# Weighting rows of experts' outputs, and half of the normalised rows, on ScalarE in a four-layer kernel

## The chip, the cores and the metric

The kernel runs on one core of one Trainium2 chip, in one launch. The metric is the device time of that launch in microseconds (us), as the median of several runs. A core has five engines with a queue each, which run in order: PE (TensorE, matrix products and transposes), DVE (VectorE), ACT (ScalarE), POOL (GpSimd) and SP (SyncE, here for issuing DMAs). They meet only through semaphores.

## What is computed

The input x has 2 sequences of 1024 tokens with 128 channels, in float32. Four layers follow each other; every one does the same thing with its own two branches:

```
xn = layernorm(x)                      # no scale, no shift
s  = mixer(xn)                         # layer 0: Mamba-2, 1: delta rule, 2: linear attention, 3: two Mamba-2, one reversed
g  = silu(experts(xn))                 # a mixture of experts
x  = x + s * g
```

The layer norm takes the mean and the variance of a token's 128 channels and gives (x - m) / sqrt(v + 1e-5). In the experts of layers 1 to 3 each token goes to the two experts with the largest logits out of 8, 8 and 16, and the result is their two outputs weighted by the softmax over these two logits. Layers 1 and 3 add a shared expert; layer 2 runs a softmax attention ahead of its experts. Layer 0 computes all 8 experts for all tokens.

## The kernel before, in words

The tokens lie in 16 tiles of 128 (one token to a partition), and four tiles make a group: G = 4, NG = 4. Arrays such as `x`, `xn`, `acc`, `h`, `s` are kept whole in SBUF as 128 partitions x 16 tiles x 128 channels; `grp(a, g)` is one group of them, 128 x 512 elements.

**Normalisation.** `Kern.normalise` (L320) does it for layers 0, 1 and 2, a loop of its own in `layer3` (L1684) for layer 3. For every group `moments` (L303) takes BATCH_NORM_STATS (L310) and BATCH_NORM_AGGREGATE (L311) per tile on DVE, which gives mean and variance in `mv`; `rsqrt` (L296) makes the reciprocal root `rs` by one small DVE operation (L299), a square root on ACT (L300), and a reciprocal on DVE (L301). Layers 2 and 3 also take mean squares (L317, L318). Then DVE writes the four rows of the group, one tile of 128 x 128 each, as (x - m) * rs (L328, in layer 3 L1688). The group is stored to a list in DRAM for the experts (`keep_rows`, L1257, on SP; layers 1 and 3), transposed by PE (L293) and copied from PSUM to `xT` by ACT or DVE in turn (L282, L284). In layer 2 ACT scales the rows for the attention (`xw`, L1381) and POOL turns them (L1389 to L1394); in layer 3 ACT scales them as `xw` (L1696), POOL copies part of that (L1697), and POOL multiplies weights (L1674) at the beginning. In layer 0 ACT takes sums of squares of the same rows (L336).

**Experts of layers 1 to 3.** `Dispatch` (L1134 on) sorts the 4096 pairs of token and expert into blocks of one expert each. The mixers' work and the blocks of rows share the engines: a block's rows are gathered from DRAM (`load`, POOL), put through its expert, and scattered to a list `ys` in DRAM (`store`, L1236, POOL), in which every token has a place for its first and one for its second expert. At the end of the layer `Dispatch.fetch` brings them back. Per group and per k (first or second expert) SP loads a tile `yt` of 128 x 4 x 128 (L1247), after all stores; four buffers take turns. Then `add_scaled` runs for each of the four rows on DVE (L414):

```
self.nc.vector.scalar_tensor_tensor(acc[:, i, :], out, w, acc[:, i, :], ALU.mult, ALU.add)
```

that is, acc = y * w + acc, with w one weight per token. `acc` holds the shared expert's output in layers 1 and 3 and `h`, the attention's, in layer 2. After `fetch` the layer's end follows for the group: a silu on ACT (L1005, L1129, L1808), a product with s on DVE (L1006, L1130, L1809), and the sum with x on DVE (L1007, L1131, L1810). In layer 3 SP then writes the output (L1811). The chunks of the state space of layer 3 (`StateSpace.unit`, L540 on: exponentials `uE` and `ueA` on ACT, products on DVE and POOL, among them L632, L640 and L597) run beside its last fetch.

**Order.** Each engine's order is made when the program is built, by a planner that runs the instructions through a model of their times and takes what is ready first. Only PE's order in the attention of layer 2 is written out by hand. Tiles come from pools; a tile of a pool that reuses memory waits for the last reader of what lay there.

Of the kernel before, what the change touches and what calls it, by code (L numbers as in the profile page):

```python
# [10 lines left out]
F32 = mybir.dt.float32  # L11
F32R = mybir.dt.float32r
I32 = mybir.dt.int32
AF = mybir.ActivationFunctionType
ALU = mybir.AluOpType
# [4 lines left out]
P = 128  # L20
# [4 lines left out]
G = 4  # L25
# [247 lines left out]
class Kern:  # L273
# [29 lines left out]
    def moments(self, pool, src, n, eps, tag):  # L303
# [8 lines left out]
        self.rsqrt(rs, mv[:, :, 1], 1.0, eps)  # L312
        return mv, rs

    def mean_squares(self, out, mv, rs):

        self.nc.vector.tensor_mul(out, mv[:, :, 1], rs)  # L317
        self.nc.vector.tensor_mul(out, out, rs)  # L318

    def normalise(self, pool, ps, x, xn, xT, xs=None, ms=None):  # L320

        for g in range(NG):
            mv, rs = self.moments(pool, lambda j: x[:, g * G + j, :], G, 1e-5, "ln")
            if ms is not None:
                self.mean_squares(ms[:, g * G : (g + 1) * G], mv, rs)
            for j in range(G):
                i = g * G + j
                self.nc.vector.tensor_scalar(xn[:, i, :], x[:, i, :], mv[:, j, 0:1], rs[:, j : j + 1], ALU.subtract, ALU.mult)  # L328
            if xs is not None:
                keep_rows(self, xs, xn, g)  # L330
            self.to_feature_major(ps, lambda i: xn[:, i, :], xT, g)
# [72 lines left out]
    def logits(self, pool, ps, xT, w, bias, E):  # L404
# [3 lines left out]
        lg = pool.tile([P, NT, E], F32, name="lg", tag="lg")  # L408
        self.nc.vector.tensor_add(lg, pl, bias.unsqueeze(1).to_broadcast([P, NT, E]))
        return lg  # L410

    def add_scaled(self, acc, i, out, w):

        self.nc.vector.scalar_tensor_tensor(acc[:, i, :], out, w, acc[:, i, :], ALU.mult, ALU.add)  # L414

# [248 lines left out]
def grp(a, g):  # L666
    return a[:, g * G : (g + 1) * G, :]
# [466 lines left out]
class Dispatch:  # L1134
# [106 lines left out]
    def fetch(self, pool, acc, g, weights):  # L1241

        nc, tc = self.K.nc, self.K.tc
        slots = self.ys.rearrange("(k i p) d -> p k i d", k=2, p=P)
        for k, wk in enumerate(weights):
            y = pool.tile([P, G, P], F32, name="yt", tag="yt", bufs=4)
            d = nc.sync.dma_start(y, slots[:, k, g * G : (g + 1) * G, :])  # L1247
            for q in self.out:
                tc.add_manual_dep(d.ins, q.ins.name, mybir.DependencyInfo(mybir.DependencyClass.Sync, mybir.DependencyReason.DATA), reason="slots of any block")
            for j in range(G):  # L1250
                i = g * G + j
                self.K.add_scaled(acc, i, y[:, j, :], wk[:, i : i + 1])


def keep_rows(K, xs, src, g):

    K.nc.sync.dma_start(xs.rearrange("(i p) d -> p i d", p=P)[:, g * G : (g + 1) * G, :], grp(src, g))  # L1257
# [396 lines left out]
def layer3(K, x, xn, xT, w, inp, out):  # L1654
    nc, tc, c = K.nc, K.tc, K.c
    four = [P, G, P]
    with ExitStack() as es:
        pa = es.enter_context(tc.tile_pool(name="a3", bufs=1))
        pf = es.enter_context(tc.tile_pool(name="f3", bufs=1))
# [21 lines left out]
        rs = pa.tile([P, NT], F32, name="ars")  # L1681
        xs = inp["lists"][0]
        pl = sf.tile([P, NT, 20], F32, name="plg", tag="ps")
        for g in range(NG):  # L1684
            mv, r = K.moments(pf, lambda j: x[:, g * G + j, :], G, 1e-5, "ln")
            for j in range(G):
                i = g * G + j
                nc.vector.tensor_scalar(xn[:, i, :], x[:, i, :], mv[:, j, 0:1], r[:, j : j + 1], ALU.subtract, ALU.mult)  # L1688
            keep_rows(K, xs, xn, g)
            gr = rs[:, g * G : (g + 1) * G]  # L1690
            K.mean_squares(gr, mv, r)
            K.rsqrt(gr, gr, 1.0, 1e-5)
            xw = tmp.tile([P, G, 192], F32, name="xw", bufs=2)
            for j in range(G):
                i = g * G + j
                nc.scalar.activation(xw[:, j, :P], xn[:, i, :], AF.Copy, scale=rs[:, i : i + 1])  # L1696
            nc.gpsimd.tensor_copy(xw[:, :, P:], xw[:, :, :64])  # L1697
            K.to_feature_major(sf, lambda i: xn[:, i, :], xT, g)
            b, l0 = g * G // TPB, g * G % TPB * P
            for swap in range(2):  # L1700
                pt = sa.tile(four, F32, name="tpx", tag="ps")
                for j in range(G):
                    nc.tensor.transpose(pt[:, j, :], xw[:, j, 64 * swap : 64 * swap + P], c["ident"])
                pt = pt.rearrange("p a b -> p (a b)")
                up, down = pt[:64], pt[64:]
                if swap:
                    m = min(512, SEQ - 1 - l0)
                    K.copy(X[0][64:, b, l0 + 3 : l0 + 3 + m], down[:, :m])
                    m = 0 if l0 else 1
                    K.copy(X[1][:64, b, l0 + m - 1 : l0 + 511], up[:, m:])  # L1710
                else:
                    K.copy(X[0][:64, b, l0 + 2 : l0 + 514], up)
                    K.copy(X[1][64:, b, l0 : l0 + 512], down)
            for i in range(g * G, g * G + G):
                K.mm(pl[:, i, :], xT[:, i * P : (i + 1) * P], wr)
# [73 lines left out]
        acc = pa.tile([P, NT, P], F32, name="acc", tag="acc")  # L1789
# [24 lines left out]
def build(tc, io, packs):  # L1814
    nc = tc.nc
    with ExitStack() as ctx:
        pool = ctx.enter_context(tc.tile_pool(name="const", bufs=1))
        x = pool.tile([P, NT, P], F32, name="x")
        src = io["x"].rearrange("b (t p) d -> p (b t) d", p=P)
        for g in range(NG):  # L1820
            nc.sync.dma_start(grp(x, g), src[:, g * G : (g + 1) * G, :])
        xn = pool.tile([P, NT, P], F32, name="xn")
        xT = pool.tile([P, T], F32, name="xT")

        def load(into, n, by=nc.scalar):
            t = into.tile([P, packs[n].n], F32, name="w_" + n)
            by.dma_start(t, io[n])
            return View(t, packs[n])

        K = Kern(tc, load(pool, "c"))  # L1830
        dram = ctx.enter_context(tc.tile_pool(name="lists", bufs=1, space=DRAM))
        lists = {n: dram.tile([rows, P], F32, name=n) for n, rows in (("xs", T), ("ys", 2 * T))}
        views = {}
        with tc.tile_pool(name="const0", bufs=1) as pool0:
            w0 = load(pool0, "l0")
            e0 = load(pool0, "e0")
            layer0(K, x, xn, xT, w0, e0)
        later = ctx.enter_context(tc.tile_pool(name="const3", bufs=1))
        views["l3"] = load(later, "l3")
        pair = lists["xs"], lists["ys"]  # L1840
        with tc.tile_pool(name="const2", bufs=1) as pool0:
            views.update((n, load(pool0, n)) for n in ("l1", "l2"))
            layer1(K, x, xn, xT, views["l1"], {"rows": io["rows1"], "lists": pair, **{n: io[n] for n in ("sw1", "sw3", "sw2")}})
            layer2(K, x, xn, xT, views["l2"], {"rows": io["rows2"], "lists": pair})
        layer3(K, x, xn, xT, views["l3"], {"load": lambda pool: load(pool, "x3", nc.sync), "rows": io["rows3"], "lists": pair}, io["out"].rearrange("b (t p) d -> p (b t) d", p=P))
# [17 lines left out]
```

## Time and profile before

| | |
|---|---|
| median of three runs | 1351.3 us (1349.75 to 1352.39) |
| the profiled execution | 1358.85 us, its span 1357.1 us |
| instructions | 19084 |
| mean granted clock of PE | 0.887 of full speed |
| busy PE / DVE / ACT / POOL | 1132.7 / 872.6 / 632.0 / 421.5 us |
| L328, rows normalised, layers 0 to 2 | 48 on DVE, 397 ns each in the mean |
| L1688, the same in layer 3 | 16 on DVE, 516 ns each in the mean |
| L414, rows weighted and added | 96 on DVE, 16 to 32 to a form, medians 339 to 343 ns |
| L1247, loads of yt | 24 of 256 KB, 3.2 us from issue to landing in the median |

The profile is that of one execution, so its time is set against its own span and not against the median. Busy is the time in which an engine executes something; an engine can be idle because it waits, and the profile gives for each group of instructions what ended the idle time ahead of it. The timeline gives, per row: start, duration, engine, line and operation, `out<-in` by the names of the tiles, shape, how many in a row, and in brackets how long the engine was idle before and what released it. Durations overlap within one engine's queue[...].

Where things lie in the span, in us: layer 0 from 0 to 219, layer 1 to 472 (its fetch from 442), layer 2 to 1108 (normalisation 477 to 497, fetch from 1090), layer 3 to the end (normalisation 1105 to 1135, fetch from 1312).

### The profile page before, as it was taken

How to read it: one execution, taken by the hardware profiler on the slowest of the kernel's cores; microseconds unless marked ns; L12 is line 12 of the kernel's file. 1: busy time of each engine (PE TensorE's matmuls, PEld its weight loads, DVE VectorE, ACT ScalarE, POOL GpSimd, SP SyncE). 2: the span in 40 equal slices, each digit the busy share in tenths (PEclk: the TensorE clock that was granted, in tenths of full speed). 3: DMA queues.
4: the chain of work that ended last, by engine and by line, in shares of the span. 5: the costliest groups of instructions: out<-in, count | busy, mean ns of one | idle time of the engine just before them, and what ended most of it. 6: DMA issues, size and time to landing. Idle time of an engine off the chain costs nothing. (4 is left out here: it accounts for less than half of the span.)

```text
span 1357.1 us, 19084 instructions
## 1 busy us (share of the span) xinstructions
PE 1132.7 (83%) x6813; PEld 790.6 (58%) x6813; DVE 872.6 (64%) x2128; ACT 632.0 (47%) x1050; POOL 421.5 (31%) x427
## 2 busy tenths in 40 slices
PE   5699876889899658999998998569989919799995
PEld 2367465788799325544444443347768815477674
DVE  6536445775664886677777661977776477665456
ACT  7664925214612342345556576234353325355661
POOL 0352161036454260000000000034766511377743
PEclk9799886799799967799999989869999958799997
DMA  2000003025344200000000000023345430233411
GB/s 90 0 0 1 1 15 116 8 88 160 99 142 107 63 0 0 1 1 1 1 1 16 9 1 1 8 91 103 127 125 160 131 105 24 70 94 104 65 53 47
DMA packets 49039, 75.71 MB, mean 56 GB/s; under 512 B 7335, under 2 KB 36402, under 8 KB 48688
## 3 DMA queue, kind: packets, MB, share of 16 engines
q1 hardware_dynamic: 39632, 54.30, 12.8%
q0 software_dynamic: 8448, 14.98, 5.0%
q10 hardware_dynamic: 864, 5.21, 1.1%
q8 instruction: 54, 0.88, 0.3%
q14 instruction: 41, 0.34, 0.1%
HBM read 63.95 MB, written 12.85 MB: 57 GB/s over the span
## 5 line engine op out<-in xcount | busy, mean ns | idle before, releaser
L1226 POOL DMA_INDIRECT xb<-xs,dfrom x132 | 132.7, 1005 | 567.9 <-DVE gsum L1291 377.1
L1453 DVE TENSOR_REDUCE mx<-pm 128x1 f32<-128x512 f32 (+3 forms) x304 | 181.9, 655 | 66.1 <-PE pm L287 63.7
L1497 ACT ACTIVATE pr<-psc 128x1024 f32<-128x1024 f32 x144 | 139.5, 1021 | 95.8 <-PE psc L287 67.3
L1236 POOL DMA_INDIRECT ys<-yb,dto x132 | 134.9, 1022 | 86.4 <-DVE yb L1124 35.5
L287 PE MATMUL pm<-kT,qT 32*128 32x128 f32 (+3 forms) x576 | 120.3, 369 | 16.2 <-DVE mx L1453 12.5
L287 PEld LDWEIGHTS pm<-kT,qT 32*128 32x128 f32 x576 | 70.2, 207 | 69.5 <-DVE mx L1453 49.0
L287 PE MATMUL p<-xbT,tw 128*128 128x256 f32 x368 | 98.4, 385 | 3.5 <-ACT sg L1117 3.2
L1117 ACT ACTIVATE sg<-p,tw 128x256 f32<-128x256 f32 x92 | 41.0, 472 | 93.6 <-PE p L287 90.5
L287 PE MATMUL pat<-pr,va 128*32 128x512 f32 x576 | 81.7, 635 | 0.2 <-ACT pr L1497 0.2
L293 PE MATMUL tp<-w_c,xn 128*128 128x128 f32 x64 | 20.5, 421 | 71.8 <-DVE xn L328 44.2
L287 PEld LDWEIGHTS p<-xbT,tw 128*128 128x128 f32 x368 | 62.3, 190 | 14.8 <-ACT sg L1117 5.5
L287 PE MATMUL psc<-qT,kT 32*128 32x512 f32 x288 | 64.7, 496 | 2.8 <-ACT pr L1497 2.7
L1118 DVE SCALAR_TENSOR_TENSOR hh<-p,tw,sg 128x256 f32<-128x256 f32 x92 | 42.3, 475 | 38.4 <-ACT sg L1117 32.9
L287 PEld LDWEIGHTS po<-tw,hh 128*128 128x128 f32 x368 | 54.2, 191 | 10.3 <-issue 3.1
L293 PEld LDWEIGHTS tp<-w_c,xn 128*128 128x128 f32 x64 | 11.8, 190 | 80.2 <-DVE xn L328 28.1
L287 PE MATMUL po<-tw,hh 128*128 128x128 f32 x368 | 56.1, 275 | 1.6 <-DVE yb L1124 1.2
L287 PE MATMUL psc<-mT,onesR 32*128 32x512 f32 x288 | 54.1, 416 | 0.0
L282 ACT COPY xbT<-pxb 128x256 f32<-128x256 f32 (+3 forms) x39 | 15.6, 399 | 64.8 <-PE pxb L813 45.7
L287 PEld LDWEIGHTS psc<-qT,kT 32*128 32x128 f32 x288 | 30.6, 191 | 15.6 <-ACT pr L1497 13.1
L287 PE MATMUL pcum<-kv,w_c 128*128 128x512 f32 x64 | 35.8, 660 | 3.5 <-DVE prod L1317 3.1
L287 PE MATMUL pd<-uda,w_c 128*128 128x512 f32 x64 | 35.2, 652 | 0.9 <-ACT usz L533 0.9
L561 POOL TENSOR_TENSOR uda<-w_c,vdA 128x512 f32<-128x512 f32 x20 | 20.6, 1041 | 48.4 <-PE pd L287 47.6
(523 smaller groups left out, 2787.3 us busy)
## 6 DMA issues: line engine op xcount, KB each, us to landing
tw<-in_rows SPq DMA_DIRECT2D x23, 836.0 KB, 4.7
tw<-in_rows SPq DMA_DIRECT2D x39, 384.0 KB, 3.6
yt<-ys SPq DMA_DIRECT2D x24, 256.0 KB, 3.2
tw<-in_rows SPq DMA_DIRECT2D x47, 128.0 KB, 2.3
xb<-xs,dfrom POOLq DMA_INDIRECT x132, 3.2
ys<-yb,dto POOLq DMA_INDIRECT x132, 2.3
xs<-xn SPq DMA_DIRECT2D x8, 256.0 KB, 2.3
w_l<-in_l ACTq DMA_DIRECT2D x1, 1890.0 KB, 11.2
```

The lines of the kernel that those rows point to most:

```text
L282: self.nc.scalar.copy(out, in_)
L287: self.nc.tensor.matmul(out, lhsT=lhsT, rhs=rhs, start=start, stop=stop)
L293: self.nc.tensor.transpose(pt[:, j, :], src(g * G + j), self.c["ident"])
L561: pool.tensor_mul(da, upto.unsqueeze(1).unsqueeze(1).to_broadcast(lay), m["dA"][:, i0 + j : i0 + j + per, :].unsqueeze(3).to_broadcast(lay))
L1117: nc.scalar.activation(sg, p1[:, k - k0, :], AF.Silu, bias=t[:, 1536 + k : 1537 + k])
L1118: nc.vector.scalar_tensor_tensor(hh[:, k, :], p2[:, k - k0, :], t[:, 1540 + k : 1541 + k], sg, ALU.add, ALU.mult)
L1226: self.K.nc.gpsimd.indirect_dma_start(dst, None, self.xs, bass.IndirectOffsetOnAxis(self.of_token[:, n : n + 1], 0))
L1236: d = self.K.nc.gpsimd.indirect_dma_start(self.ys, bass.IndirectOffsetOnAxis(self.to[:, n : n + 1], 0), src, None, bounds_check=2 * T - 1, ...
L1453: nc.vector.tensor_reduce(mx[:, starts.index(a), g, j : j + k], tile[0][:, : k * m].rearrange("p (j m) -> p j m", m=m), AX.X, ALU.max)
L1497: K.nc.scalar.activation(pr, ps, AF.Exp, scale=scale)
```

## The change

A new function `normal_rows` writes a group's rows. It first makes `off` = -m * rs, a tile of 128 x 4, on DVE. Rows 0 and 2 of the group stay on DVE as before. Rows 1 and 3 go to ACT, as Identity with the scale rs and the bias off, one value each per partition. It serves all four layers.

In `fetch` ACT now multiplies each of the four rows of `y` by its weight, in place, and one DVE addition of 128 x 512 adds the whole tile to the group of acc. `add_scaled` goes.

```diff
+    def normal_rows(self, pool, xn, x, g, mv, rs):
+
+        nc = self.nc
+        off = pool.tile([P, G], F32, name="lnoff", bufs=2)
+        nc.vector.scalar_tensor_tensor(off, mv[:, :, 0], -1.0, rs, ALU.mult, ALU.mult)
+        for j in range(G):
+            i = g * G + j
+            if j % 2:
+                nc.scalar.activation(xn[:, i, :], x[:, i, :], AF.Identity, bias=off[:, j : j + 1], scale=rs[:, j : j + 1])
+            else:
+                nc.vector.tensor_scalar(xn[:, i, :], x[:, i, :], mv[:, j, 0:1], rs[:, j : j + 1], ALU.subtract, ALU.mult)
...
@@ normalise
-            for j in range(G):
-                i = g * G + j
-                self.nc.vector.tensor_scalar(xn[:, i, :], x[:, i, :], mv[:, j, 0:1], rs[:, j : j + 1], ALU.subtract, ALU.mult)
+            self.normal_rows(pool, xn, x, g, mv, rs)
...
-    def add_scaled(self, acc, i, out, w):
-
-        self.nc.vector.scalar_tensor_tensor(acc[:, i, :], out, w, acc[:, i, :], ALU.mult, ALU.add)
...
@@ Dispatch.fetch
             for j in range(G):
                 i = g * G + j
-                self.K.add_scaled(acc, i, y[:, j, :], wk[:, i : i + 1])
+                nc.scalar.activation(y[:, j, :], y[:, j, :], AF.Copy, scale=wk[:, i : i + 1])
+            nc.vector.tensor_add(grp(acc, g), grp(acc, g), y)
...
@@ layer3
-            for j in range(G):
-                i = g * G + j
-                nc.vector.tensor_scalar(xn[:, i, :], x[:, i, :], mv[:, j, 0:1], r[:, j : j + 1], ALU.subtract, ALU.mult)
+            K.normal_rows(pf, xn, x, g, mv, r)
```

## The prediction, made before the changed kernel ran

> **What bounds the kernel now.** I read the page first (PE busy 83% of the span, DVE 64%, ACT 47%), then the chain of waits. That chain can be followed back only to 1104 us, about 19% of the span, so for the rest I read each place that the change touches by itself: first the busy time by stage, then the timeline inside the stage. The changed lines run in seven stages: the normalisations of layers 0 to 3 (L328, L1688) and the fetches of layers 1 to 3 (L414). Columns: stretch, its length, then busy us of PE, PEld, DVE, ACT, POOL, then granted clock, DMA share, GB/s.
>
> ```profile
> 0.00:40.00 40.00, 24.65 (x74) 12.28 (x74) 27.02 (x92) 27.44 (x71) 2.38 (x9) 0.96 0.23 76
> 222.00:245.00 23.00, 17.20 (x58) 13.30 (x59) 15.19 (x71) 18.05 (x42) 0.00 (x0) 0.57 0.49 169
> 449.00:472.00 23.00, 13.53 (x64) 8.23 (x64) 20.66 (x54) 7.47 (x12) 4.40 (x5) 0.96 0.17 47
> 478.00:500.00 22.00, 9.55 (x27) 5.36 (x28) 18.34 (x75) 9.29 (x29) 13.18 (x20) 0.50 0.00 0
> 1090.00:1109.00 19.00, 0.00 (x0) 0.00 (x0) 15.14 (x53) 3.14 (x5) 0.14 (x2) 0.50 0.56 172
> 1109.00:1136.00 27.00, 18.42 (x84) 15.79 (x84) 20.35 (x75) 13.16 (x37) 9.77 (x11) 0.57 0.14 40
> 1312.00:1337.00 25.00, 18.70 (x129) 14.38 (x128) 22.07 (x59) 10.68 (x16) 8.63 (x7) 0.93 0.37 106
> ```
>
> The three fetches (449, 1090, 1312) and the normalisations of layers 2 and 3 (478, 1109) are DVE's: it is busy 75 to 90% of them, ACT 17 to 49%. The normalisations of layers 0 and 1 are not: ACT is at 18.05 of 23 us in layer 1, and in layer 0 it runs from 18.4 to 40 us almost without a gap. The timeline of layer 1 shows what it does there, and who waits:
>
> ```profile
> 236.34 1.28 ACT L874 ACT_TABLE_LOAD   x1
> ...
> 242.63 0.69 DVE L885 TENSOR_TENSOR vb<-vb,beta 128x512 f32<-128x512 f32 x1 [1.14 <-ACT beta L877]
> ```
>
> The tail, from the last fetch to the end, in the timeline:
>
> ```profile
> 1315.53 1.14 DVE L414 SCALAR_TENSOR_TENSOR acc<-yt,rw,acc 128x128 f32<-128x128 f32 x4 [2.62 <-DMA yt<-ys]
> ...
> 1329.73 2.40 DVE L414 SCALAR_TENSOR_TENSOR acc<-yt,rw,acc 128x128 f32<-128x128 f32 x4
> ...
> 1333.89 0.73 DVE L632 SCALAR_TENSOR_TENSOR uy<-uxs,w_l,py 128x512 f32<-128x512 f32 x1
> ...
> 1334.77 1.98 PE L287 MATMUL py<-uE,uxdt 128*64 128x128 f32 x16 [3.23 <-DVE uy L632]
> ```
>
> DVE stands 2.6 us for the first fetched rows, then runs without a gap to 1336; its L414 rows stand in front of uy L632, and PE waits 3.23 us for that one on the way to the end.
>
> **What each operation costs.** From the groups by form (mean ns in the fourth place from the end):
>
> ```profile
> L414 DVE SCALAR_TENSOR_TENSOR h<-yt,rw,h 128x128 f32<-128x128 f32 x16 | 4.7, 344 | 7.2 <-DMA yt<-ys 7.2
> L1006 DVE TENSOR_TENSOR acc<-acc,WT 128x512 f32<-128x512 f32 x4 | 2.8, 692 | 2.3 <-ACT acc L1005 2.3
> L1696 ACT ACTIVATE xw<-xn,ars 128x128 f32<-128x128 f32 x16 | 5.1, 391 | 1.7 <-DVE ars L301 1.5 <-DVE lnrs L301 0.2
> L516 ACT ACTIVATE uxs<-px,w_l 128x512 f32<-128x512 f32 x16 | 12.1, 778 | 0.7 <-PE px L287 0.6
> L478 ACT ACTIVATE uxs<-px,w_l 128x512 f32<-128x512 f32 x24 | 16.3, 687 | 17.0 <-PE px L287 16.9
> ```
>
> Instructions of one engine overlap, so in a queue the distance counts. Four L414 rows take 1.14 us: (1.14-0.34)/3 = 0.265 each. Four L1696 rows take 1.28 us: 0.295 each. The group's add is L1006's shape: 0.69 alone, 0.60 in a row (L1131 at 1099.80, next instruction at 1100.40). A normalised row on DVE is 0.26 (four L328 in 1.11). The same row on ACT, with scale and bias per partition, is not in the trace: L1696 has one such operand, and a second costs 0.09 (L516 against L478), so 0.48 alone and 0.385 in a row. It could be as low as L1696's 0.295; I take 0.385.
>
> Here a rule speaks against the change. The Trainium skill, ScalarE: Activation LUTs, Rules for kernel authors, gives multiplying and adding to VectorE, not ScalarE. By the rows it is right on price: 0.295 against 0.265, so a layer's 32 weightings cost ACT 9.4 us where DVE paid 8.5. By the rule the change loses wherever ACT is full, 0.9 us a layer and the adds on top. By the stages, ACT has 14 to 16 us idle in each fetch, and what counts is what DVE no longer does.
>
> **Fetch, layers 1 to 3.** Per layer DVE loses 32 x 0.265 = 8.5 us and gets 8 adds x 0.60 = 4.8: 3.7 less. ACT gets 9.4. No DMA is added. A yt buffer is held until the add (about 1.28+0.7 us after landing instead of 1.14), so the later four of eight loads on SP's queue are issued about a microsecond later.
> Layer 1: nothing in the stage waits for yt (issued at 442.13, median landing 3.2, first used at 449.27), ACT is 32% busy, and DVE goes on after x at 472.36 with casts that wait for nothing else. So the saving passes on, less new waits of adds for ACT: **-3.0**, from 0 to -3.7.
> Layer 2: DVE runs from 1093.47 to 1108.3, 14.8 us, and layer 3 starts behind it. Now ACT sets the pace: 32 x 0.295 + three silus at 0.55 = 11.1, then add 0.7, silu 0.7, mul 0.7, add 0.7: 14.0. The last yt loads, held longer, may add some: **-0.5**, from -1.5 to +1.5.
> Layer 3: the same 3.7 from a DVE that is full from 1315.5 to 1336, at the end of which PE waits for L632. On ACT the scalings stand ahead of exps, silus and copies of the state space, and wait for the landing that DVE now waits 2.6 us for. Next late behind DVE is POOL's uE product, which ends at 1331.5, some 2.4 us before L632 starts. So **-2.5**, from -3.7 to +1.
>
> **Normalisation.** Per group of four rows DVE loses 2 x 0.26 and gets the offset: L317's shape, 0.09 in a row. That is 0.43 less, 1.7 a layer; ACT gets 2 x 0.385, 3.1 a layer. The rows on ACT wait for the offset, and whatever ACT has behind them (copies, sums of squares, table loads) waits too.
> Where POOL works, DVE's rows are dearer:
>
> ```profile
> 1111.74 3.04 DVE L1688 TENSOR_SCALAR xn<-x,lnmv,lnrs 128x128 f32<-128x128 f32 x4
> 1112.39 1.80 POOL L1674 TENSOR_TENSOR bwst<-w_x 128x768 f32<-128x768 f32 x1
> ```
>
> Four rows take 3.04 instead of 1.11, with one L1674 on POOL from 1110.63 and this one behind it. The Trainium skill, SBUF — State Buffer, Who interferes with whom, says that such a DVE operation and a POOL operation exclude each other, that an operation with two SBUF inputs is caught too while POOL reads, and that ACT never waits. By the first and last points the two ACT rows are worth up to (3.04-1.11)/2 = 1.0 us a group here. By the middle one the offset itself, through which both ACT rows go, is caught: L318 of that size took 0.71 at 490 us. I go by that row, and take less than half.
> Layer 2: the rows of groups 2 and 3 take 3.6 and 2.7 us (487.9, 493.9) between POOL's rotations; two fewer save up to 1.5 and 0.7 after the offset. DVE is the stage's engine and PE waits for its rows: **-1.5**, from -2.5 to +0.5.
> Layer 3: group 0 is held by the two L1674 either way, group 2 (1.99 us) gains 0.8, the others 0.2 each; ACT's xw rows come 0.8 later per group: **-0.5**, from -2 to +2.
> Layer 1: six rows fall into ACT's gap-free stretch, 2.3 us; half of it is covered, as PE's last transposes (242.15) stand behind its logits anyway: **+1.2**, from 0 to +2.3. If that cover goes, it is the whole 2.3.
> Layer 0: the same, with the first group waiting for data at 5.4 and 9.9 us, and DVE's convolutions ending the stretch: **+0.5**, from -0.5 to +2.3.
>
> **Sum:** -3.0-0.5-2.5-1.5-0.5+1.2+0.5 = -6.3 us. The profiled execution took 1358.85 us (span 1357.1), 7.6 above the median of the runs, 1351.3. The difference goes over unscaled: 1352.5 on the profiled execution, **1345.0** on the median. The order within each queue is made by a planner from its own durations, and new instructions can shift it anywhere outside layer 2's hand-ordered PE stretch; I give that 3 us either way, most of this forecast's own range, 1341 to 1348.6. About 0.2%, 2.7 us, is what a measurement here can tell from no change.
>
> **Rivals.**
> (B) All of DVE's time shows, POOL's hold on the rows as well: -3.7-3.7-0.8-2.5-1.5 with layers 0 and 1 at nothing, -12.2: 1339. For it: DVE's 90% in two fetches. Against: ACT's pace in layer 2, and the latency of two engines in place of one. 0.10.
> (C) The saving is hidden: next late is the landing of yt, ACT's silu, or POOL's product, and the ACT terms cancel the rest: 1351, within 2.7. For it: DVE already waits 2.3 us for silu in layer 1's fetch. Against: no DMA wait there at all. 0.22.
> (D) Slower: ACT's queue becomes the bound. Its place is the gap-free stretches of layers 0 and 1 (+2.3 each), layer 3's xw rows (+1.5), layer 2's fetch (+1.5), and the tail, where a scaling waits up to 2.6 us for yt with the exps and copies of the state space behind it (+1.0 net); layer 1's fetch and layer 2's normalisation still give -1.5-1.0. Sum +6.1: 1357.4. It decides from the point where the ACT terms pass the 8.0 us that my DVE terms give. Against it: 51 to 83% of ACT idle in five of seven stages, and Copy and Identity rows that stand in the trace behind other functions with no table load. 0.20.
> The forecast has 0.48. Faster is B and the forecast, 0.58; same 0.22; slower 0.20. The range, 1339 to 1356.5, leaves out half of B and a good part of D.
>
> **What would show it.** DVE's busy time falls by some 18 us (3 x 3.7 + 4 x 1.7), ACT's rises by about 40 with the same number of table loads. From the first yt use to x the fetch of layer 1 shortens by 3, that of layer 2 by under 1; PE's wait for L632 shrinks. Layer 1's normalisation to its first DVE wait for beta lengthens by about 1. I am wrong if ACT waits for yt with state-space work behind it, if table loads multiply, or if a stretch that the change doesn't touch moves by more than 3 us.

## The result, and the profile after

The changed kernel is slower: 1364.57 us in the median of 15 runs (1360.7 to 1372.02), against 1355.1 us (1349.64 to 1363.55) for the kernel before in 15 runs taken with it. The ratio is 1.007 with an interval of [1.0051, 1.0089]. The forecast was 1345.0 us, and its range ended at 1356.5. It started from 1351.3 us for the kernel before, the median of three runs; against the 1355.1 of this comparison the change costs 9.5 us, where 6.3 us less was forecast.

The profiled execution of the changed kernel took 1363.79 us, its span 1362.0 us (before: 1358.85 and 1357.1). Its line numbers are shifted: in layer 1's and 3's fetch L1258 is the weighting on ACT and L1259 the group's add on DVE; L323 is a normalised row on ACT. From its page, the busy time per engine and the chain that ended last by engine:

```profile
PE 1136.2 (83%) x6813; PEld 789.4 (58%) x6813; DVE 854.8 (63%) x2040; ACT 667.2 (49%) x1175; POOL 420.9 (31%) x427
...
PE 55%; DVE 19%; ACT 14%; issue 5%; POOL 4%; DMA 3%; SPq 0%; DVEq 0%; POOLq 0%; ACTq 0%
```

DVE lost 17.8 us of busy time and ACT gained 35.2, close to the 18 and 40 of the prediction (three table loads of 1.28 us fewer are part of the difference in ACT's). So the work went where it was meant to go, at about the price that was put on it. The groups by form of the changed kernel say the same:

```profile
L1258 ACT ACTIVATE yt<-yt,rw 128x128 f32<-128x128 f32 x48 | 15.2, 389 | 12.9 <-DMA yt<-ys 12.9
L323 ACT ACTIVATE xn<-x,lnoff,lnrs 128x128 f32<-128x128 f32 x32 | 14.0, 484 | 4.3 <-DVE lnoff L319 4.3
```

The first line also shows 12.9 us in which ACT stood idle for the landing of `yt`. Most of it, 9.35 us, is in layer 2's fetch, where ACT has nothing else to do; 3.18 us are in layer 1's and 0.34 us in layer 3's, and there other work of ACT stands behind these rows.

Where the time went, in us, by stretches between named instructions of the two traces. `TT` is the first triangular factor of layer 1 (DVE), `pk` layer 2's first key product, `px` layer 3's first state-space product, `pinv` the product from which `Dispatch` takes its list of places (the last three PE):

| stretch | before | after | predicted | measured |
|---|---|---|---|---|
| layer 1 normalisation (last x of layer 0 to the first TT) | 34.36 | 30.96 | +1.2 | -3.4 |
| layer 1 fetch (first yt load to the last x) | 30.23 | 34.44 | -3.0 | +4.2 |
| layer 2 normalisation (first statistics to the first pk) | 20.54 | 19.34 | -1.5 | -1.2 |
| layer 2 attention | 289.17 | 291.77 | 0 | +2.6 |
| layer 2 fetch (last ys store to the last x) | 20.03 | 19.85 | -0.5 | -0.2 |
| layer 3 normalisation (x to the first px) | 28.13 | 26.57 | -0.5 | -1.6 |
| layer 3, px to the last pinv | 30.54 | 32.58 | 0 | +2.0 |
| layer 3 tail (first yt load to the last x) | 41.02 | 44.80 | -2.5 | +3.8 |

The spans differ by +4.9. The table adds up to some +6.3, layer 0 as a whole is 2.2 us shorter (217.4 against 219.6, forecast +0.5), and the rest differs by under a microsecond. The two stretches with the wrong sign are the fetches of layers 1 and 3. First their busy time by stage, of the kernel before (columns as in the prediction):

```profile
442.10:472.40 30.30, 20.18 (x96) 12.14 (x94) 25.23 (x73) 10.88 (x19) 5.56 (x5) 0.96 0.25 70
...
1312.50:1353.50 41.00, 27.58 (x168) 22.91 (x166) 29.10 (x77) 13.58 (x20) 13.56 (x10) 0.79 0.23 67
```

and of the changed one:

```profile
436.30:470.70 34.40, 22.97 (x95) 13.85 (x93) 21.80 (x49) 22.46 (x53) 5.27 (x5) 0.90 0.22 62
...
1313.60:1358.40 44.80, 30.21 (x176) 24.30 (x175) 26.53 (x53) 23.67 (x53) 14.29 (x11) 0.80 0.21 61
```

DVE (third pair) is busy 3.4 and 2.6 us less, about the 3.7 forecast, and yet each stretch is longer. No engine is busy throughout: ACT (fourth pair) is at 65% and 53%. So engines wait, and the timeline must show for what. Layer 1's fetch, before:

```profile
445.09 1.28 ACT L300 ACT_TABLE_LOAD   x1
...
446.62 0.18 DVE L301 RECIPROCAL lors<-lors 128x4 f32<-128x4 f32 x1 [2.23 <-ACT lors L300]
...
449.27 1.96 DVE L414 SCALAR_TENSOR_TENSOR acc<-yt,rw,acc 128x128 f32<-128x128 f32 x4
```

and after:

```profile
439.08 1.28 ACT L1258 ACTIVATE yt<-yt,rw 128x128 f32<-128x128 f32 x4 [2.18 <-DMA yt<-ys]
...
441.82 0.57 ACT L856 ACTIVATE sg<-pgt 128x512 f32<-128x512 f32 x1
442.41 1.28 ACT L300 ACT_TABLE_LOAD   x1
...
443.94 0.18 DVE L301 RECIPROCAL lors<-lors 128x4 f32<-128x4 f32 x1 [5.41 <-ACT lors L300]
...
446.90 1.28 ACT L856 ACT_TABLE_LOAD   x1
...
448.81 1.28 ACT L300 ACT_TABLE_LOAD   x1
```

The first load of `yt` is issued at 436.27. In the kernel before, its first reader ran 7.1 us after the issue (442.13 to 449.27), and 4.3 us after the landing (444.96). In the changed kernel the planner puts the first weighting on ACT 2.8 us after it, so ACT stands 2.18 us for the landing, then weights eight rows, and only then come the shared expert's silu (`sg`) and the square root of the delta rule's last norm. DVE waits 5.41 us for that root instead of 2.23. From there the order of silus and roots on ACT alternates: after 442.41 it loads a function table three times more (446.90, 448.81, 450.32), where before it did so once (449.61).

The tail, in the kernel before. ACT's copy `uBt` feeds PE's state product `pst`; the state space's output products `py` come behind it:

```profile
1320.67 0.59 ACT L588 COPY uBt<-pt 128x512 f32<-128x512 f32 x1 [0.64 <-PE pt L583]
...
1322.26 0.61 PE L287 MATMUL pst<-uxst,uBt 128*128 128x128 f32 x4
...
1324.94 1.02 PE L287 MATMUL pgt<-xT,w_l 128*128 128x512 f32 x2
...
1329.58 1.09 PE L287 MATMUL py<-uE,uxdt 128*64 128x128 f32 x16
```

and after:

```profile
1321.89 1.27 ACT L1258 ACTIVATE yt<-yt,rd 128x128 f32<-128x128 f32 x4
1323.06 0.56 ACT L594 COPY uBt<-pt 128x512 f32<-128x512 f32 x1
...
1327.60 0.57 ACT L594 COPY uBt<-pt 128x512 f32<-128x512 f32 x1
...
1328.26 1.19 PE L287 MATMUL pst<-uxst,uBt 128*128 128x128 f32 x4 [4.04 <-ACT uBt L594]
...
1334.01 1.92 PE L287 MATMUL pgt<-xT,w_l 128*128 128x512 f32 x2
...
1337.76 1.09 PE L287 MATMUL py<-uE,uxdt 128*64 128x128 f32 x16
```

Before, the second `uBt` ran as soon as PE had its input (1320.64). After, that input is there at 1321.44 and the copy runs at 1327.60, 6.2 us late, with weightings and silus in front of it on ACT. PE stands 4.04 us for it, and its clock falls with the wait, as two slices of the tail show, one ahead of the wait and one behind it (the granted clock is third from the end):

```profile
1318.60:1323.60 5.00, 4.63 (x31) 3.43 (x29) 2.14 (x3) 4.97 (x14) 2.49 (x2) 1.00 0.35 106
...
1328.60:1333.60 5.00, 3.55 (x15) 2.96 (x15) 5.00 (x13) 3.71 (x12) 2.95 (x2) 0.50 0.35 105
```

The kernel before has a granted clock of 1.00 in the whole of 1312.5 to 1332.5. The pair of `pgt` products takes 1.92 us instead of 1.02. `py` starts 24.1 us after the first load instead of 17.1. The 7.0 us shrink to 3.8 at the end, since before PE waited 3.23 us for L632 next, which it now doesn't; behind that wait its clock was lower too (0.62 in 1332.5 to 1337.5, then 0.50).

### The profile page after: what moved, and what is told of

Same layout as the page of the kernel before. It is cut to its first block, busy times and chain, and to the rows that moved or that the text cites. A ratio compares the mean times of both kernels' runs of the same rounds, so it can differ in the third digit from the quotient of the medians.

```text
span 1362.0 us, 19140 instructions
## 1 busy us (share of the span) xinstructions
PE 1136.2 (83%) x6813; PEld 789.4 (58%) x6813; DVE 854.8 (63%) x2040; ACT 667.2 (49%) x1175; POOL 420.9 (31%) x427
## 4 chain that ended last, share of the span: by engine, by line
PE 55%; DVE 19%; ACT 14%; issue 5%; POOL 4%; DMA 3%; SPq 0%; DVEq 0%; POOLq 0%; ACTq 0%
PE pm L287 6%; DVE mx L1460 5%; PE pat L287 5%; PE p L287 4%; PE po L287 3%; PE px L287 3%; PE psc L287 3%; PE pcum L287 2%; PE pob L287 2%; PE pgb L287 2%; PE pq L287 1%; PE pyo L287 1%; PE pU L287 1%; ACT yt L1258 1%; PE pd L287 1%
## 5 line engine op out<-in xcount | busy, mean ns | idle before, releaser
L526 DVE SCALAR_TENSOR_TENSOR uxs<-uxr,w_l,uxs 128x512 f32<-128x512 f32 x48 | 34.4, 758 | 1.9 <-ACT uxr L282 1.7
```

Of the source, the lines that this page charges most:

```text
L526: nc.vector.scalar_tensor_tensor(xs[:, k, :], xr[:, k, at : at + W], m["cw"][:, k, t : t + 1], xs[:, k, :], ALU.mult, ALU.add)
```

## The experiments

Theory: the place of the weightings in ACT's queue costs the time (rival D's mechanism, in the fetches); the same instructions behind the urgent ones would cost nothing. Rivals: W, ACT's pace, the work itself, costs it, wherever it stands; R, the planner's new order in stretches that the change doesn't touch costs it. The three sets below ran on three chips, whose absolute times differ, so every ratio is against the kernel before on the same chip. (On which chip the comparison above ran is not on record.)

**Set 1, the change by parts** (before: 1357.11).

e1_norm_only is the changed kernel with the fetch as before:

```diff
-                nc.scalar.activation(y[:, j, :], y[:, j, :], AF.Copy, scale=wk[:, i : i + 1])
-            nc.vector.tensor_add(grp(acc, g), grp(acc, g), y)
+                nc.vector.scalar_tensor_tensor(acc[:, i, :], y[:, j, :], wk[:, i : i + 1], acc[:, i, :], ALU.mult, ALU.add)
```

> Only the normalisation is changed; the fetch weights on VectorE as before. Theory Q (ScalarE's in-order queue at the fetches costs the time, the normalisation gains): 2 to 6 us faster than the kernel before, ratio 0.996 to 0.999, layer 1's normalisation 4 to 8 us shorter as in the changed kernel. Rival R (the planner's new order in stretches that the change does not touch costs the time): also slower, ratio over 1.002. Rival of the prediction (ScalarE full in layers 0 and 1): slower by 2 to 5 us with the loss inside layers 0 and 1.

Measured: 1351.18 us, 0.9955 [0.9935, 0.9975]. Normalisation doesn't cost; its stretches move by -2.4, -1.2 and -2.0 in layers 1, 2 and 3. The 4 to 8 us expected of layer 1's did not come in full.

e2_fetch_only is the reverse, the kernel before with only the fetch of the changed one.

> Only the fetch is changed, in all three layers. Theory Q: 8 to 14 us slower, ratio 1.006 to 1.010, with the fetch of layer 1 some 4 us longer, the tail of layer 3 some 4 us longer, layer 2's fetch within 1 us, the rest of the loss small. Rival R: the total differs from that by more than 4 us, and not in the fetches.

Measured: 1370.91 us, 1.0089 [1.0058, 1.0119]. So the loss comes with the fetch's edit, but not all of it in the fetches. By stretches: fetch of layer 1 +4.3, tail +3.3, and also +3.8 in the experts of layer 2 and +2.0 in px to pinv, which the edit doesn't touch. In the tail PE waits for `uBt` twice, 4.9 us in sum, the longer wait 4.03.

e3_fetch_l1 and e4_fetch_l3 split that once more. The condition of e3, below, holds in layer 1 alone; in e4 it is `self.E == 16`, which is layer 3:

```diff
+            if self.E == 8 and self.R == P:
+                for j in range(G):
+                    i = g * G + j
+                    nc.scalar.activation(y[:, j, :], y[:, j, :], AF.Copy, scale=wk[:, i : i + 1])
+                nc.vector.tensor_add(grp(acc, g), grp(acc, g), y)
+            else:
...
+                    self.K.add_scaled(acc, i, y[:, j, :], wk[:, i : i + 1])
```

> The fetch is changed in layer 1 alone. Theory Q: 3 to 5 us slower (ratio 1.002 to 1.004), all of it between the first load of the fetched rows and the last sum of the layer. Rival R: that stretch is longer by less than 2 us, or the total moves by another amount than the stretch by over 3 us.

Measured: 1360.7 us, 1.0018 [1.0002, 1.0033]. The fetch of layer 1 is +3.7 in its own stretch. Layer 2's experts go from 175.48 to 179.35, where all engines have another order than before between 850 and 1040 us, and layer 3's normalisation from 28.13 to 24.97. So R is real here: with one layer's fetch changed, layer 2's experts became 3.9 us longer. (Layer 3's normalisation got another order too, but that stretch also differs by 1.5 us between two profiles of one kernel: 26.57 in the changed one, 25.09 in a2 below.) In e2 the experts have this new order as well and take 179.32. In the changed kernel they have the old one and take 175.47, so there it isn't the cause.

> The fetch is changed in layer 3 alone. Theory Q: 3 to 5 us slower (ratio 1.002 to 1.004), all of it after the first load of the fetched rows, with TensorE waiting for the copy uBt behind the weightings on ScalarE. Rival R: nothing before the fetch should differ, so no change, or a change elsewhere.

Measured: 1360.58 us, 1.0026 [1.0008, 1.0044], +3.5 us; its tail is 44.92 against 41.02, and PE waits 4.0 us for `uBt`. DVE, ACT and POOL have the order of the kernel before up to the tail, so the tail alone accounts for it. By their medians e3 and e4 together give 7.1 us of e2's 13.8. e2 is longer than e3 in layer 3's normalisation (28.64 us against 24.97) and in px to pinv (32.54 against 30.72), neither of which the edit touches. Layer 2's fetch was not run alone; in e2 its stretch is 20.1 us against 20.0.

**Set 2, the place in the queue** (before: 1405.05).

q1_pinned is the changed kernel with the same instructions, but the weightings of layer 1 stand behind the shared expert's last silu and those of layer 3 behind the last `uBt` copy (`behind` fixes an order on one engine):

```diff
-                nc.scalar.copy(Bt, pt)
+                K.bt = nc.scalar.copy(Bt, pt)
...
+                inp["sg"] = nc.scalar.activation(sg, pgt, AF.Silu)
...
+                op = nc.scalar.activation(y[:, j, :], y[:, j, :], AF.Copy, scale=wk[:, i : i + 1])
+                if first is not None:
+                    self.K.behind(op, first)
...
+            d.fetch(pe, acc, g, w12, K.bt)
```

> The whole change, but the weightings on ScalarE are put, in the planned order, behind the shared expert's last silu in layer 1 and behind the state space's last copy uBt in layer 3. Same instructions, other place in the queue. Theory Q (what stands behind the weightings pays): layer 1's fetch, 34.4 us in the changed kernel, comes to 30 or less, the tail, 44.8, to 41.5 or less, and the total is 6 to 10 us under the changed kernel. Rival W (the weightings' own work and the second hop between engines cost the time, wherever they stand): both stretches stay over 33.5 and 44, or lengthen, since the work is bunched at the end.

Measured: 1405.16 us, 1.0000 [0.9982, 1.0018]. Of Theory Q's three figures the tail's came (38.82 us), layer 1's did not (32.39), and the total, set against a2 next, fell by less.

a2_after_again is the changed kernel as it is, on the same chip.

> The changed kernel once more, for the spread of its stages between two profiles and for its time beside the other three. The fetches should repeat within 0.5 us (layer 1 34.4, layer 2 19.8, tail 44.8), the total within its interval, 1.005 to 1.009. A stage without a change of order that differs by 2 us or more between the two profiles is spread, not effect.

Measured: 1409.87 us, 1.0043 [1.0026, 1.0059]. So moving the weightings within ACT's queue takes 4.7 us off, with the same arithmetic; two table loads fall away in layer 1's fetch (125 in the kernel for 127). The planner also ordered other stretches anew, so the sum need not be the pin's alone. Its own places are these: the tail goes from 44.07 (a2) to 38.82 (q1). In layer 1 it goes only from 33.73 to 32.39, and the timeline of q1 shows why:

```profile
466.39 0.60 ACT L856 ACTIVATE sg<-pgt 128x512 f32<-128x512 f32 x1 [0.28 <-PE pgt L287]
466.88 1.26 ACT L1258 ACTIVATE yt<-yt,rw 128x128 f32<-128x128 f32 x4
```

The first weighting now comes 18.5 us after the first load (448.34), and from it to the end of the stage ACT has 32 rows and four silus one after the other. There W is right: pinned too late, ACT's pace sets the end.

a2 also shows what two profiles of one kernel differ by (perhaps with the chip). The fetches repeat within 0.7 us (33.73, 20.13 and 44.07 against 34.44, 19.85 and 44.80). Layer 1's normalisation takes 28.36 us against 30.96, and layer 2's attention 287.84 against 291.77. So the +2.6 of the attention in the table above is spread, and the -3.4 of layer 1's normalisation hardly more than that.

n01_norm_l0_l1 and n23_norm_l2_l3 have the new normalisation in two layers each, and the fetch as before. In n01 it is the two layers without mean squares, as below; in n23 the condition is `ms is not None`, and layer 3 has the new rows too:

```diff
+            if ms is None:
+                self.normal_rows(pool, xn, x, g, mv, rs)
+            else:
...
+                    self.nc.vector.tensor_scalar(xn[:, i, :], x[:, i, :], mv[:, j, 0:1], rs[:, j : j + 1], ALU.subtract, ALU.mult)
```

> Only the normalisation of layers 0 and 1 is changed. The recorded prediction: slower by 1.7 us, as ScalarE is full there. The other theory (the rows leave a VectorE that has four more uses for the time, and ScalarE's table loads cover them): faster by 1 to 4 us, with the stretch from layer 0's last sum to the first triangular factor of layer 1 shorter by 2 us or more.

> Only the normalisation of layers 2 and 3 is changed. The recorded prediction: faster by 2.0 us, 1.5 of it in layer 2. By the profile of the normalisation alone: layer 2's stretch from its first statistics to its first key product shorter by 1.2 us, layer 3's from the last sum to the first state-space product by 2, faster by 3 to 4 us. If the order elsewhere decides: the stretches shorten and the total doesn't.

Measured: 1403.46 us, 1.0001 [0.9985, 1.0017], and 1405.62 us, 0.9995 [0.9969, 1.0021]. The stretches got shorter (layer 1's normalisation 29.14 us in n01; layer 2's 19.34 and layer 3's 27.05 in n23), and the totals didn't. Neither half gives anything that can be told from nothing, so e1's gain isn't placed by them. And the new order of layer 2's experts, which went with 3.9 us in set 1, costs nothing on this chip: 183.12 us in q1 and 183.77 in n23, which have it, against 184.00 in a2 and 183.63 in n01, which have the old one.

**Set 3, what is worth keeping** (before: 1402.69).

q3_tail_pinned is the kernel before with only the tail's weightings on ACT, behind the last `uBt`:

```diff
+                if first is None:
                     nc.vector.scalar_tensor_tensor(acc[:, i, :], y[:, j, :], wk[:, i : i + 1], acc[:, i, :], ALU.mult, ALU.add)
+                else:
+                    self.K.behind(nc.scalar.activation(y[:, j, :], y[:, j, :], AF.Copy, scale=wk[:, i : i + 1]), first)
+            if first is not None:
+                nc.vector.tensor_add(grp(acc, g), grp(acc, g), y)
```

> The kernel before, with only layer 3's fetch on ScalarE, put behind uBt. It differs from the run with layer 3's fetch alone (tail 44.9) only in the place in the queue. Theory Q: tail 38.5 to 39.5, total 1 to 3 us under the kernel before. Rival W: tail 42 or more, total above the kernel before.

Measured: 1402.51 us, 1.0000 [0.9977, 1.0023]. Its tail is 38.69, where e4, with the same work unpinned, has 44.92. The timeline of q3 has the order that makes the difference:

```profile
1361.97 0.58 ACT L588 COPY uBt<-pt 128x512 f32<-128x512 f32 x1
1362.44 1.28 ACT L1255 ACTIVATE yt<-yt,rw 128x128 f32<-128x128 f32 x4
```

Against 40.12 of e1b, which has the old tail on the same chip, that is 1.4 us less, and against 41.02 of the kernel before's profile 2.3. PE waits nowhere for `uBt` there. The total doesn't show it; its interval is 3 us to either side.

q4_by_group is q1 with layer 1's group n (1 to 4) behind the silu 4+n of eight, instead of all behind the last.

> The whole change; layer 1's weightings of the first, second, third and fourth group stand behind the shared expert's fifth to eighth silu, where behind the last they took 32.4 us; layer 3 as in the run behind uBt. Theory Q: layer 1's fetch at 30 or less, under the 30.2 of the kernel before, as VectorE has 3.7 us less to do. Rival W: 31 to 34, the second hop and ScalarE's pace bind whatever the place.

Measured: 1401.46 us, 0.9974 [0.9951, 0.9998]. Layer 1's fetch takes 30.16: what the misplacing cost is gone, and what DVE saves there (3.7) still doesn't show against the 30.23 of before. The whole change, placed so, comes out at 0.9974 of the kernel before, where the same arithmetic in the planner's own order came out at 1.007 and 1.0043.

b1_norm_tail joins e1's normalisation with q3's tail; fetches of layers 1 and 2 stay on DVE.

> A version meant to be faster: the normalisation of the change, the fetch on VectorE as before in layers 1 and 2, and in layer 3 on ScalarE but put behind uBt in the planned order. Theory Q: the tail, 41.0 us before and 44.8 with the change, comes to 39; the total is 2 us under the normalisation alone, 4 to 9 us under the kernel before (0.993 to 0.997). Rival W: tail over 41, no faster than the normalisation alone.

Measured: 1397.52 us, 0.9954 [0.9933, 0.9974], with a tail of 38.81. This version beats the kernel before by more than its uncertainty, and the changed one with it (1.0043 and 1.007); it isn't told apart from e1.

e1b_norm_again is e1 once more, beside it.

> The normalisation alone once more, beside the others: in one set it gave 0.9955 together, in another its two halves gave 1.0001 and 0.9995. If the gain is the sum of the shortened stretches (layer 1 3, layer 2 1, layer 3 1 to 2 us): 0.995 to 0.998. If the shortened stretches are given back later: 0.999 to 1.001.

Measured: 1400.51 us, 0.9984 [0.9965, 1.0003], so e1's 0.9955 was not found again in full.

## Why the prediction was wrong

**Prices: right.** DVE's fall, ACT's rise, 0.48 for a normalised row on ACT (484 ns) and the pace of the weightings (four in 1.27 us) came as estimated. So did the offset's: beside POOL's work it took 0.73 us (at 489.26), in layer 2's other three groups 0.15 to 0.16.

**Fetch of layer 1, -3.0: the step that failed.** What stands behind the moved rows in ACT's queue was put at nothing. "Nothing in the stage waits for yt ... So the saving passes on." The first half was read from an order that the change itself undid. The slack of 7.1 us between load and first use was DVE's place for L414 and no property of the data; on ACT the planner placed the rows next in the queue 2.2 us before they had landed, ahead of `sg` and `lors`. The stage came out at +4.2, in e3 alone at +3.7. With the rows moved by group behind the silus (q4), it is level with before: 30.16 us, where the profiles with the fetch on DVE have 30.05 to 31.07. So even in a better place the term was about zero and not -3.0; what takes up DVE's 3.7 us there was not pursued.

**Tail, -2.5: the second step that failed, a wait that the sum left out.** The prediction saw that "the scalings stand ahead of exps, silus and copies of the state space" and put +1.0 on it only in rival D; its own sum follows DVE and POOL to L632 and has no term for PE's wait for `uBt`. The runs showed +3.8, +3.3 (a2 against n01, which has the old tail, on the same chip) and +3.9 (e4). Behind `uBt` the same work gives 38.7 to 38.8, 1.4 to 2.3 us below the old one: much of the -2.5 was there to be had, in another order. The missed price was PE's: one wait of 4.0 us for `uBt` in the changed kernel, e2, e4 and a2 alike, and behind it products at a lower clock.

In the pair of profiles the two terms together are 13.5 us off (+8.0 measured, -5.5 forecast), more than the whole forecast (+4.9 for -6.3), as the normalisations gave more than their term. The 3 us that the prediction gave the planner's order either way were too few.

**Fetch of layer 2, -0.5:** -0.2 in the pair of profiles, and +0.15 between the means of all profiles with and without ACT's rows there (20.02 against 19.87), where half a microsecond was forecast. The picture of it was right: ACT runs without a gap from 1093.71 to 1104.76, 11.05 us for the 11.1 of the sum.

**Normalisation, -0.3 in sum (layers 0 to 3: +0.5, +1.2, -1.5, -0.5).** Means over the profiles that have the new rows and those that have the old: layer 1 31.3 against 33.2 us, but from 28.4 to 34.7 and from 31.2 to 34.6, so the two overlap; layer 2 19.6 against 20.5, without overlap; layer 3 26.5 against 27.6, overlapping again. The loss in the "gap-free stretch" of ACT in layer 1 did not come. Layer 0's front, from the start to its first `uxdt`, is 86.2 against 86.0.

**The rivals.** B (12.2 us faster) and C (no change) did not come. D's sign was right, and it named the tail; it also named five places (layers 0 and 1, layer 3's xw, layer 2's fetch) where nothing was lost, and counted layer 1's fetch as a gain. It came out on the right side for a part of its reasons. The rule of the Trainium skill (ScalarE: Activation LUTs, Rules for kernel authors) that multiplying belongs on VectorE pointed the right way, but not by the price measured here: 0.29 against 0.265 us a row would have been under a microsecond a layer.

**Its signs of error.** "ACT waits for yt with state-space work behind it" is what the tail shows, though there the weightings' own time (6.6 us for sixteen rows with a table load and an exponential among them) weighs more than the wait of 0.34 us. In e4 ACT waits for no landing of `yt` ahead of the last `uBt`, and the tail is +3.9 all the same: there it is the rows' place that costs, not the landing. Table loads multiplied only locally, two more in layer 1's fetch (the whole kernel has 127 against 130); whether these two cost anything by themselves was not tried apart.

**What stays open.** The medians differ by 9.5 us in one comparison and by 4.8 on the chip of set 2 (a2; its ratio gives 6.0), and the profiles by 4.9. In the pair of profiles the fetches of layers 1 and 3 are +8.0, the normalisations of layers 1 to 3 -6.2, layer 0 -2.2, and two untouched stretches +4.6. Layer 2's attention (287.8 to 295.0 in all profiles) and the stretch from px to pinv (30.1 to 32.8) move without a pattern in what was changed, and were not pursued. The size of the normalisation's gain lies between nothing and 6 us.

## What to carry to other kernels

Moving work to an idle engine is priced by what will stand behind it in that engine's in-order queue, not by the engine's idle share: ask for each moved instruction what data it waits for and which copy or root of another chain comes next. Slack read from a trace belongs to the old order; when the reader moves to another engine, the slack must be read again. Where an order is planned, pin the moved work behind the last urgent instruction of its engine, piece by piece and not all behind one, since both too early (a2) and too late (q1, layer 1) cost.

## What was not expected of the hardware

The kernel before took 1355.1 and 1357.11 us in two comparisons and 1405.05 and 1402.69 us in two others, these two on chips other than that of the 1357.11. The difference isn't even: in the profiles of all kernels the experts of layer 3 take 139 to 142 us on the one side and 170 to 177 on the other, those of layer 2 175 to 179 and 183 to 185; most other stretches agree within a few microseconds. Why was not looked into. And a wait of PE can cost more than its length: behind the 4.04 us the granted clock stood at 0.50 for the next 5 us, where it had been 1.00 ahead of it, and a pair of products took 1.92 us instead of 1.02. In a2 it is the same: 0.50 in the 5 us behind a wait of 4.03.
